# Gate products of a gated graph network: one Strassen–Winograd step in fp32, or three float32r products of split operands

## The chip, the cores and the metric

The kernel runs on one core of one Trainium2 chip. The metric is the device time of one execution in microseconds; the kernel before the change takes 2126.82 us, the median of 3 runs (2126.05 to 2127.76).

## What is computed

There are 128 graphs of 128 nodes with 256 features each. Two layers follow one another, both with a residual. Cut to what matters:

```
h = relu(layernorm(x))                          # first layer: gated graph network
A = (adj != 0)
for i in 0..2:                                  # three rounds
    aggr = A^T @ (h @ weight[i])
    gi = aggr @ w_ih.T + b_ih ; gh = h @ w_hh.T + b_hh      # 768 columns: r, z, n
    r = sigmoid(gi_r + gh_r) ; z = sigmoid(gi_z + gh_z)
    n = tanh(gi_n + r * gh_n)
    h = (1 - z) * n + z * h
x = x + h
h = relu(layernorm(x))                          # second layer: graph attention
Wh = h @ W.T
att = softmax over j of leaky_relu(Wh@a1 [i] + Wh@a2 [j]) where adj, else 0
out = x + att @ Wh
```

The "gate products" are gi and gh. The kernel multiplies `weight[i]` into `w_ih` once, at the start, so a round needs (A^T h) times a product matrix and h times `w_hh`.

## The kernel before, in words

Four graphs form a group (G = 4, T = 512 node columns), so there are 32 groups of three rounds, and a **step** is one round of one group. State is kept turned, as `hT`: 2 chunks of 128 features by 512 columns. The 96 steps are in an order written out at the end (`plan`, L1152), sorted by 3·group + STEP·round with STEP = 4, so that two to three steps of other groups lie between two rounds of one group. The last step of all is done in two halves of 256 columns.

What a step does on each engine:

- **gather** (`inputs`, L647, and `gathered`, L630): the state in rows, `h`, times the mask A gives `pa` in PSUM: 8 fp32 products of 128 columns; ScalarE copies `pa` to `aT` (L663).
- **moving sums** (`moving_sums`, L484): VectorE makes the four Winograd sums of `hT` and of `aT`, 8 operations of 128x256 (L493).
- **gate products** (`gru_step`, L710): the 256x256 products are cut in 2x2 blocks and done with 7 block products in place of 8 (`blocks`, L749, and `product`, L723). A step has two phases (reset gate with the hidden half of the new state; update gate with the given half). Each phase has 7 products of 3 matmuls, so a step issues 42 fp32 matmuls of 128x128 by 256 columns, all on L737. Between the products ScalarE copies PSUM banks (L757, L760, L770) and VectorE adds them (L763, L774).
- **gates**: tanh and scaling on ScalarE from PSUM (L795, L802, L830), additions on VectorE (L837, L682), tanh of the new state (L688), then the new state in three VectorE operations of 128x1024 (L694, L696, L698).
- **rows**: the next gather needs the state in rows. Where more than two steps lie between rounds, VectorE transposes 32x32 blocks and SyncE's queue moves them through DRAM (`to_rows_by_blocks`, L581, `by_way_of_dram`, L538); otherwise TensorE transposes (`rows`, L618, `to_rows`, L519).

After the third round the `epilogue` (L940) does the attention of that group: `pq` (L637) and `po` (L1124) on TensorE and the rest on the other engines. The `prologue` (L905) normalises a group's input.

The order of all instructions is set when the program is built. `Order` (L173) keeps a time for each engine; work that is not a gate product waits as tasks, each with an assumed length, and `fill`, `fixed` and `matmuls` place the tasks around the products. Once placed, each engine runs its instructions in that order and waits for what they need. SyncE issues every DMA (L60).

At the start the product matrices are computed (`given_weights`, L368) and their Winograd sums made (`stationary_sums`, L328).

Of the kernel before, what the change touches and what calls it, by code (L numbers as in the profile page):

```python
# [8 lines left out]
F32 = mybir.dt.float32  # L9
I32 = mybir.dt.int32  # L10
# [13 lines left out]
BIG = 1e30  # L24


@with_exitstack
def preln_gnn_kernel(
# [33 lines left out]
    XT, AT = 3, 2  # L62
    ROWS = 6
# [6 lines left out]
    def load_adjacency(g):  # L70
        at = io.tile([P, G, P], I32, tag="at", name=f"at_{g}", bufs=AT)
        dma(at, adj[g * G : (g + 1) * G].rearrange("b s t -> s b t"))
        return at
# [15 lines left out]
    def two_chunks(pool, tag, name, **bufs):  # L89
        return [borrowed(pool, [P, C, T], tag, f"{name}_{k}", 3 * D, **bufs) for k in range(C)]  # L90

    wih = two_chunks(work, "hs", "wih")
    whh = two_chunks(gate, "v", "whh")
# [7 lines left out]
    def load_weight(l, pool, shape, tag):  # L101
        w = borrowed(pool, shape, tag, f"wt_{l}", C * D)
        w = w.rearrange("p (c d) -> p c d", d=D)
        dma(w, weight_t[l].rearrange("(c p) d -> p c d", p=P))
        wt.append(w)


    load_weight(0, gate, [P, 2, H], "m")
    load_gates(wih, w_ih_t, slice(0, 1))
# [3 lines left out]
    xts, ats = {0: (xt_0, (4.8, 5.8))}, {}  # L113
    load_gates(wih, w_ih_t, slice(1, 3))
    ats[0] = load_adjacency(0), 8.6
    load_gates(whh, w_hh_t, slice(0, 1))
    load_gates(whh, w_hh_t, slice(2, 3))
    load_gates(whh, w_hh_t, slice(1, 2))
    load_weight(1, work, [P, G, P], "e")
    load_weight(2, work, [P, G, P], "e")  # L120
# [7 lines left out]
    gw = borrowed(work, [P, G, P], "prT", "gw", C * D).rearrange("p (c f) -> p c f", f=D)  # L128
# [3 lines left out]
    for g in range(2, XT):  # L132
        xts[g] = load_rows(g), 18.0 + 2.0 * g
# [6 lines left out]
    c1 = [ps_sum.tile([P, 2, H], F32, name=f"c1_{n}") for n in range(2)]  # L140
    c2 = ps_sum.tile([P, 2, H], F32, name="c2")
    u = ps_sum.tile([P, 2, H], F32, name="u")
    m7 = ps_sum.tile([P, 2, H], F32, name="m7")
    for bank in (*c1, c2):
        bank = bank.rearrange("p g t -> p (g t)")
        put(nc.tensor.matmul(bank, zero[:, 0:P], zero, start=True, stop=True))
# [24 lines left out]
    more = u, m7, c2, *c1  # L171

    class Order:  # L173
        def __init__(self):
            self.free = dict.fromkeys((PE, ACT, DVE, POOL, SP, "port"), 0.0)
            self.tasks = []

            self.rooms = {room: [0.0] * 2 for room in ("tq", "x1", "prT", "e", "hs")}
            self.rooms |= {"misc": [0.0] * 3, "h": [0.0] * ROWS}
            self.next, self.room_of = dict.fromkeys(self.rooms, 0), {}  # L180
# [37 lines left out]
        def open(self, room, name):  # L218
            self.room_of[name] = room, self.next[room]
            self.next[room] = (self.next[room] + 1) % len(self.rooms[room])  # L220
            if room == "misc" and self.room_of[name][1] > 2:

                return more[self.room_of[name][1] - 3].rearrange("p n t -> p (n t)")
            if room == "misc":
                return ps_misc.tile([P, T], F32, tag="misc", name=name)
            if room == "h":
                return work.tile([P, G, D], F32, tag="h", name=name, bufs=ROWS)
# [4 lines left out]
            return work.tile([P, C, T], F32, tag=room, name=name)  # L232
# [90 lines left out]
    S1, S2, S3, S4, N22, W11, W12 = range(7)  # L323

    def stationary_tile(name):
        return const.tile([P, 3, 7, P], F32, name=f"s_{name}")

    def stationary_sums(s, into, w, gates, ready):  # L328


        v = [wk.rearrange("p (g o m) -> p g o m", g=3, o=2) for wk in w]
        w11, w21 = v[0][:, gates, 0, :], v[0][:, gates, 1, :]
        w12, w22 = v[1][:, gates, 0, :], v[1][:, gates, 1, :]
        n = gates.stop - gates.start
        eng = nc.vector
        long, short = 0.05 + 0.15 * n, 0.05 + 0.12 * n

        def done(block, t):
            for gate_no in range(gates.start, gates.stop):
                into[gate_no, block] = t  # L340

        t = yield DVE2, long, ready
        put(eng.tensor_tensor(s[:, gates, S3, :], w11, w21, ALU.subtract))
        done(S3, t)
        t = yield ACT, 0.1 + 0.14 * n, ready
        put(nc.scalar.copy(s[:, gates, W11, :], w11))
        done(W11, t)
        t1 = yield DVE2, long, ready
        put(eng.tensor_tensor(s[:, gates, S1, :], w21, w22, ALU.add))
        done(S1, t1)  # L350
        t = yield ACT, 0.1 + 0.14 * n, ready
        put(nc.scalar.copy(s[:, gates, W12, :], w12))
        done(W12, t)
        t2 = yield DVE2, long, t1 - HOP
        put(eng.tensor_tensor(s[:, gates, S2, :], s[:, gates, S1, :], w11, ALU.subtract))
        done(S2, t2)
        t = yield DVE, short, ready
        put(eng.tensor_scalar(s[:, gates, N22, :], w22, -1.0, None, ALU.mult))
        done(N22, t)
        t = yield DVE2, long, t2 - HOP  # L360
        put(eng.tensor_tensor(s[:, gates, S4, :], w12, s[:, gates, S2, :], ALU.subtract))
        done(S4, t)

    def hidden_weights(gates):
        for g, ready in gates:
            yield from stationary_sums(s_hh[0], s_hh[1], whh, slice(g, g + 1), ready)

    def given_weights(l, wf, pieces):  # L368


        for gates, ready in pieces:
            n = gates.stop - gates.start
            cols = slice(gates.start * D, gates.stop * D)
            for c in range(C):
                t = yield PE, 0.86 * n, ready, "misc"
                pw = order.open("misc", f"pw_{l}_{c}_{gates.start}")
                for k in range(C):
                    put(nc.tensor.matmul(  # L378
                        pw[:, 0 : n * D], wt[l][:, k, c * P : (c + 1) * P], wih[k][:, cols],
                        start=(k == 0), stop=(k == C - 1),  # L380
                    ))
                t = yield (ACT, 0.07 + 0.28 * n, t) if c else (DVE, 0.08 + 0.3 * n, t)
                order.close(f"pw_{l}_{c}_{gates.start}", t)
                if isinstance(wf[0], tuple):
                    wf[:] = [
                        borrowed(pool, shape, tag, f"wf_{l}_{k}", 3 * D, bufs=bufs)
                        for k, (pool, shape, tag, bufs) in enumerate(wf)
                    ]
                copy = nc.scalar.copy if c else nc.vector.tensor_copy
                put(copy(wf[c][:, cols], pw[:, 0 : n * D]))  # L390
            yield from stationary_sums(s_f[l][0], s_f[l][1], wf, gates, t)
# [9 lines left out]
    def score_weights(ready):  # L401
# [15 lines left out]
        t = yield PE, 0.5, t, "misc"  # L417
        pr = order.open("misc", "pw_r")
# [42 lines left out]
    def norm_apply(src, graphs, rstd, nb, ready, name, kept, room="h"):  # L461

        for k in graphs:
            t = yield (ACT, 0.5, ready) if kept else (ACT, 0.5, ready, room)
            if not kept:
                h = order.open(room, f"h_{name}")
                if room == "tq":
                    h = h.rearrange("p c t -> p (c t)").rearrange("p (k d) -> p k d", d=D)
                kept.append(h)
# [6 lines left out]

    def columns_tile(tag, name):
        return work.tile(
            [P, C, T], F32, tag=tag, name=f"{tag}_{name}", bufs=7 if tag == "hT" else 2
        )  # L480

    T1, T2, T3, T4 = range(4)

    def moving_sums(X, into, ready, name, parts):  # L484


        t = work.tile([P, 4, H], F32, tag=f"t{name[0]}", name=f"t_{name}")
        sums = [t[:, i, :].rearrange("p (a w) -> p a w", a=parts) for i in range(4)]
        x = X.rearrange("p c (a n w) -> p c a n w", a=parts, n=2)
        x11, x21, x12, x22 = (x[:, c, :, n] for n in range(2) for c in range(2))  # L490
        for i, one, other in ((T3, x22, x12), (T1, x12, x11), (T2, x22, sums[T1]), (T4, sums[T2], x21)):
            into[i] = t, (yield DVE2, 0.34, ready)
            put(nc.vector.tensor_tensor(sums[i], one, other, ALU.subtract))  # L493

    def to_columns(h, ready, name):
# [11 lines left out]
        for c, pt in enumerate(banks):  # L507
            t = yield ACT, 0.57, ready
            order.close(f"pt_{name}_{c}", t)
            if hT is None:  # L510
                hT = columns_tile("hT", name)
# [46 lines left out]
    def to_columns_by_blocks(h, ready, name):  # L558
# [14 lines left out]
        def place():  # L573
            nonlocal hT
            hT = columns_tile("hT", name)
            return hT.rearrange("p c t -> p (c t)")

        t = yield from by_way_of_dram(tmp.rearrange("p q n a -> p (q n) a"), place, C * G, t, name)
        return hT, t

    def to_rows_by_blocks(hT, ready, name):  # L581

        tmp = None
        for c in range(C):
# [8 lines left out]
            ))  # L593
        h = None
# [23 lines left out]
    def rows(s, ready, name):  # L618
# [3 lines left out]
        for half, pt in enumerate(banks):  # L622
            t = yield (ACT, 0.57, ready) if half else (ACT, 0.57, ready, "h")
            order.close(f"pr_{name}_{2 * half}", t)
            if h is None:
                h = order.open("h", f"h_{name}")
# [20 lines left out]
    def inputs(s, ready):  # L647

        name = f"{s.g}_{s.l}"
        s.tH, s.tA = {}, {}  # L650
        parts = len(s.parts())
        s.hidden = order.add(0, moving_sums(s.hT, s.tH, ready, f"h_{name}", parts))
        if s.l and not s.by_blocks():
            s.h, s.h_ready = yield from rows(s, ready, name)
        banks, ready = yield from gathered(s.h, s.A, s.h_ready, f"pa_{name}")
        order.close(f"h_{name}" if s.l else f"h_a{s.g}", ready)
        aT = None
        for c, pa in enumerate(banks):
            t = yield ACT, 0.57, ready
# [630 lines left out]
```

## Time and profile before

| what | value |
|---|---|
| median of 3 runs | 2126.82 us (2126.05 to 2127.76) |
| the profiled execution's own span | 2124.5 us |
| TensorE busy, weight loads busy | 2116.6 us, 1886.8 us |
| VectorE busy, ScalarE busy | 1733.1 us, 1301.4 us |
| first gate product starts | 16.21 us |
| granted clock, mean | 1.000 |

"Busy" is the share of time in which at least one instruction of the engine was running, so the durations of instructions that overlap add up to more. One fp32 matmul stands as two records in this trace, each with its own weight load. A record's duration includes the time until its last column has passed, which overlaps the next record; what one costs in a stream is the distance between starts, called its pitch below.

### The profile page before, as it was taken

To read this page: it belongs to the slowest core of one execution; us is meant where nothing else is said; L and a number is where in the kernel's file an instruction comes from. 1 tells how busy PE (TensorE), PEld (TensorE's weight loads), DVE (VectorE), ACT (ScalarE), POOL (GpSimd) and SP (SyncE) were. 2 spreads that over 40 slices of the span, in tenths; PEclk is the share of its full clock that TensorE was granted. 3 is DMA by queue.
4 is the path that set the end of the run, shared out by engine and by line. 5 is a ranking of instruction groups with operands and counts; after the bars stand their busy time and mean duration, and the time that the engine had idled before them with its cause. 6 is when DMAs were issued, how large, how long until landed. Compare 5 with 4: busy or idle time off the path is not lost.

```text
span 2124.5 us, 32340 instructions
## 1 busy us (share of the span) xinstructions
PE 2116.6 (100%) x10865; PEld 1886.8 (89%) x10865; DVE 1733.1 (82%) x3771; ACT 1301.4 (61%) x2875; POOL 126.5 (6%) x200
## 2 busy tenths in 40 slices
PE   9999999999999999999999999999999999999999
PEld 7888888888888888888888888888888888888888
DVE  7778888888878888888888888888888888787777
ACT  5556666566656666666656666666666566665666
POOL 1000000000000000000000000000000000000000
PEclk9999999999999999999999999999999999999999
DMA  5334454554455444545344554445453544444311
GB/s 159 65 85 88 86 118 107 107 117 92 98 115 119 84 96 107 122 109 113 83 108 104 117 122 82 98 106 123 110 107 88 107 107 105 96 98 94 70 31 46
DMA packets 667975, 211.95 MB, mean 100 GB/s; under 512 B 578336, under 2 KB 644640, under 8 KB 667808
## 3 DMA queue, kind: packets, MB, share of 16 engines
q1 hardware_dynamic: 667808, 209.87, 44.3%
q8 instruction: 86, 1.41, 0.3%
q14 instruction: 81, 0.66, 0.1%
HBM read 121.91 MB, written 87.88 MB: 99 GB/s over the span
## 4 chain that ended last, share of the span: by engine, by line
PE 98%; DVE 1%; ACT 0%; DMA 0%; issue 0%; POOL 0%; SPq 0%; ACTq 0%; DVEq 0%
PE c L737 35%; PE u L737 35%; PE m L737 12%; PE pa L637 8%; PE po L1124 5%; PE pq L637 2%; PE pw L378 0%; DMA xt<-in_x 0%; PE c L1124 0%; PE u L1124 0%; ACT v L688 0%; PE c L637 0%; PE pr_o L527 0%; DVE st_a L440 0%; PE pr L527 0%; ACT e L1065 0%
## 5 line engine op out<-in xcount | busy, mean ns | idle before, releaser
L830 ACT ACTIVATE z<-c,brz 128x256 f32<-128x256 f32 (+1 forms) x388 | 186.2, 480 | 328.4 <-PE c L737 186.4
L737 PE MATMUL u<-t_h,s_hh 128*128 128x256 f32 (+1 forms) x1164 | 345.0, 378 | 0.9 <-DVE c L763 0.5
L737 PE MATMUL u<-t_a,s_f 128*128 128x256 f32 (+1 forms) x1164 | 312.3, 377 | 0.0
L737 PE MATMUL c<-aT,s_f 128*128 128x256 f32 (+1 forms) x1164 | 312.3, 377 | 0.0
L795 ACT ACTIVATE r<-c,brz 128x256 f32<-128x256 f32 (+1 forms) x388 | 175.3, 475 | 194.3 <-PE c L737 112.8
L763 DVE TENSOR_TENSOR c<-u,m 128x512 f32<-128x512 f32 (+1 forms) x194 | 134.6, 694 | 140.8 <-PE u L737 140.4
L737 PEld LDWEIGHTS u<-t_h,s_hh 128*128 128x128 f32 x1164 | 218.4, 190 | 31.3 <-ACT c L757 1.6
L737 PEld LDWEIGHTS c<-aT,s_f 128*128 128x128 f32 x1164 | 220.4, 190 | 28.9
L737 PEld LDWEIGHTS u<-t_a,s_f 128*128 128x128 f32 x1164 | 220.4, 190 | 29.0
L737 PE MATMUL c<-hT,s_hh 128*128 128x256 f32 (+1 forms) x780 | 229.8, 376 | 0.0
L837 DVE TENSOR_TENSOR v<-v,c 128x256 f32<-128x256 f32 (+1 forms) x388 | 153.6, 415 | 66.3 <-PE c L737 43.7
L770 ACT COPY c<-u 128x512 f32<-128x512 f32 (+1 forms) x194 | 109.7, 566 | 117.5 <-PE u L737 116.1
L760 ACT COPY m<-m 128x512 f32<-128x512 f32 (+1 forms) x194 | 112.7, 581 | 107.1 <-PE m L737 106.9
L802 ACT ACTIVATE v<-c,bhn 128x256 f32<-128x256 f32 (+1 forms) x388 | 173.0, 474 | 0.0
L737 PE MATMUL m<-t_h,s_hh 128*128 128x256 f32 (+1 forms) x582 | 172.3, 378 | 0.0
L737 PE MATMUL c<-t_h,s_hh 128*128 128x256 f32 (+1 forms) x582 | 172.1, 377 | 0.0
L737 PEld LDWEIGHTS c<-hT,s_hh 128*128 128x128 f32 x780 | 147.6, 190 | 19.2
L774 DVE TENSOR_TENSOR c<-u,m 128x512 f32<-128x512 f32 (+1 forms) x194 | 131.8, 679 | 37.9 <-ACT c L770 34.9
L737 PE MATMUL u<-aT,s_f 128*128 128x256 f32 (+1 forms) x582 | 156.2, 377 | 0.0
L737 PE MATMUL m<-t_a,s_f 128*128 128x256 f32 (+1 forms) x582 | 156.1, 377 | 0.0
L737 PE MATMUL c<-t_a,s_f 128*128 128x256 f32 (+1 forms) x582 | 156.1, 377 | 0.0
L757 ACT COPY c<-u 128x512 f32<-128x512 f32 (+1 forms) x194 | 109.8, 566 | 43.7 <-PE u L737 43.7
(164 smaller groups left out, 3928.4 us busy)
## 6 DMA issues: line engine op xcount, KB each, us to landing
z<-tq SPq DMA_DIRECT2D x248, 128.0 KB
h<-z SPq DMA_DIRECT2D x248, 128.0 KB
xt<-in_x SPq DMA_DIRECT2D x31, 512.0 KB
z_a<-tq_a SPq DMA_DIRECT2D x120, 128.0 KB
hT_a<-z_a SPq DMA_DIRECT2D x120, 128.0 KB
z_b<-tq_b SPq DMA_DIRECT2D x116, 128.0 KB
h_b<-z_b SPq DMA_DIRECT2D x116, 128.0 KB
x<-in_x SPq DMA_DIRECT2D x29, 512.0 KB
```

What stands on the lines that cost most here:

```text
L637: put(nc.tensor.matmul(pa[:, k * P : (k + 1) * P], h[:, k, c * P : (c + 1) * P], A[:, k, :], start=True, stop=True,))
L737: put(nc.tensor.matmul(to(q), S[0][:, gate_no, weight, :], moving, start=first and q == 0 and i == 0, stop=(i == len(ends) - 1), skip_grou ...
L757: put(nc.scalar.copy(c1[0][:, :, 0:W], u[:, :, 0:W]))
L760: put(nc.scalar.copy(m[:, :, 0:W], m7[:, :, 0:W]))
L763: put(nc.vector.tensor_tensor(c2[:, :, 0:W], u[:, :, 0:W], m[:, :, 0:W], ALU.add))
L770: put(nc.scalar.copy(c1[1][:, :, 0:W], u[:, :, 0:W]))
L774: put(nc.vector.tensor_tensor(c22[:, :, 0:W], u[:, :, 0:W], m[:, :, 0:W], ALU.add))
L795: put(nc.scalar.activation(r[:, o, cols], src, AF.Tanh, bias=brz[:, o : o + 1], scale=0.5))
L802: put(nc.scalar.activation(v[:, o, cols], src, AF.Identity, bias=bhn[:, o : o + 1], scale=0.5))
L830: put(nc.scalar.activation(z[:, o, cols], src, AF.Tanh, bias=brz[:, C + o : C + o + 1], scale=0.5))
L837: put(nc.vector.tensor_tensor(v[:, o, cols], v[:, o, cols], src, ALU.add))
L1124: put(nc.tensor.matmul(po[:, j, :], hs[:, c, k * P : (k + 1) * P], gwt[:, c, :], start=(c == 0), stop=(c == C - 1),))
```

## The change

The gate products are no longer done with the Winograd sums. Each operand is split in an upper part (rounded to float32r by scaling with 1 − 2⁻¹³ on the write), a rest, and a third plane ("apart") that combines both. For each of weights and states there are three planes, and a product is the sum of three float32r products: upper by upper, rest by rest and apart by apart, the first two summed in one PSUM bank, scaled by 1 + 2⁻¹² on the way to a second bank, where the third is added. The weights' planes are made once at the start, the states' planes in each step.

A step has eight blocks of 128 output features by 512 columns; four of them take both hidden and given operand. Each use of an operand is 3 planes by 2 chunks, so a step issues 72 float32r matmuls of 512 columns (L775 of the new kernel).

Around this: STEP goes from 4 to 2, the state in rows is always made by TensorE transposes (L499), at most 4 groups are open in place of 6, input rows are prefetched 2 deep in place of 3, the mask is made in the tile that the adjacency lands in, and tiles come from counted rooms. The third plane of a block is issued behind the first two planes of the next block (`order.behind`). Cut to its core:

```diff
-    XT, AT = 3, 2
-    ROWS = 6
+    XT, AT = 2, 2
+    COLUMNS, MASKS, PLANES = 4, 4, 10
+    ROWS = {"ha": 1, "hr": 1, "h": 2}
...
-    def stationary_sums(s, into, w, gates, ready):
+    def stationary_planes(s, into, k, src, gates, ready, bank=None, factor=1.0):
...
+        put(nc.scalar.activation(upper, src, AF.Copy, scale=BELOW * factor))
...
+        put(nc.vector.scalar_tensor_tensor(
+            apart, src, factor, upper.bitcast(F32), ALU.mult, ALU.subtract
+        ))
...
+        put(nc.vector.tensor_scalar(rest, apart.bitcast(F32), 1.0 / UNIT, None, ALU.mult))
...
+        put(nc.vector.scalar_tensor_tensor(
+            apart, upper.bitcast(F32), -UNIT, apart.bitcast(F32), ALU.mult, ALU.add
+        ))
...
-    def moving_sums(X, into, ready, name, parts):
...
+    def split_rest(into, name, upper, t, whole):
...
+        put(nc.vector.scalar_tensor_tensor(
+            apart, into[REST][0].bitcast(F32), -1.0 / UNIT, upper.bitcast(F32), ALU.mult, ALU.add
+        ))
...
+    def state_planes(s, into, name):
...
+            put(nc.scalar.activation(upper[:, c, :], hT[:, c, :], AF.Copy, scale=BELOW))
...
+            put(nc.vector.tensor_tensor(rest, hT, upper.bitcast(F32), ALU.subtract))
...
+    def sum_planes(s, into, name):
...
+        banks, ready = yield from gathered(s.h, s.A, s.h_ready, f"pa_{name[3:]}")
...
+            put(nc.scalar.activation(upper[:, c, :], pa, AF.Copy, scale=BELOW))
...
+                put(nc.vector.tensor_tensor(
+                    rest[:, c, :], pa, upper[:, c, :].bitcast(F32), ALU.subtract
+                ))
...
-                    put(nc.tensor.matmul(
-                        to(q), S[0][:, gate_no, weight, :], moving,
...
+                    passes += [(weight[:, k, i, out], tile_x[:, k, cols]) for k in range(C)]
+            for i, (weight, moving) in enumerate(passes):
+                put(nc.tensor.matmul(
+                    to, weight, moving,
+                    start=first and i == 0, stop=i == len(passes) - 1, skip_group_check=True,
+                ))
...
+        def finish_block(block, i, ready):
...
+            done = product(
+                gate_no, o, ends_of[ends], (APART,), bank, False, ready,
...
+                put(nc.vector.scalar_tensor_tensor(
+                    tile_["v"][:, o, cols], tile_["r"][:, o, cols], 1.0, gates_[i][:, 0:W], ALU.add, ALU.mult
+                ))
...
+        BLOCKS = (
+            (NEW, 0, "h"), (RESET, 0, "ha"), (NEW, 1, "h"), (RESET, 1, "ha"),
+            (UPDATE, 0, "ha"), (UPDATE, 1, "ha"), (NEW, 0, "a"), (NEW, 1, "a"),
+        )
...
+            done = product(
+                gate_no, o, ends_of[ends], (UPPER, REST), sums[b][:, 0:W], True, order.free_sum[b],
...
+            if by_dve:
+                t = order.fixed(DVE, add_t, max(ready, tile_["half", o]))
+                put(nc.vector.scalar_tensor_tensor(
+                    to, bank, 1.0 + UNIT, tile_["v"][:, o, cols], ALU.mult, ALU.add
+                ))
+            else:
+                t = order.take(ACT, copy_t, ready)
...
-    STEP = 4
+    STEP = 2
...
-    LIVE = 6
+    LIVE = 4
```

## The prediction

> **What bounds the kernel now.** I read the summary of the page first, then the chain of work that ended last, then single stretches.
>
> ```profile
> PE 2116.6 (100%) x10865; PEld 1886.8 (89%) x10865; DVE 1733.1 (82%) x3771; ACT 1301.4 (61%) x2875; POOL 126.5 (6%) x200
> ```
>
> TensorE is busy all the time. A busy matmul row alone doesn't prove a bound, since records overlap, so the chain must say it:
>
> ```profile
> PE 98%; DVE 1%; ACT 0%; DMA 0%; issue 0%; POOL 0%; SPq 0%; ACTq 0%; DVEq 0%
> PE c L737 35%; PE u L737 35%; PE m L737 12%; PE pa L637 8%; PE po L1124 5%; PE pq L637 2%; PE pw L378 0%; DMA xt<-in_x 0%; PE c L1124 0%; PE u L1124 0%; ACT v L688 0%; PE c L637 0%; PE pr_o L527 0%; DVE st_a L440 0%; PE pr L527 0%; ACT e L1065 0%
> ```
>
> 98% of the chain is TensorE, 82% the gate products of L737. The pitch comes from the chain over 899 to 960 us (start, length, what):
>
> ```profile
> 918.34 1.29 PE u L737 x6
> 919.64 1.78 PE pa L637 x16
> 921.42 1.30 PE m L737 x6
> 922.72 1.78 PE pq L637 x16
> ...
> 928.39 2.59 PE c L737 x12
> 930.98 1.73 PE po L1124 x8
> ```
>
> No gap between the pieces. Twelve records of L737 take 2.59 us: 215.8 ns each, 431.6 ns for one fp32 matmul of 256 columns (two records). A 128-column record costs 1.78 / 16 = 111 ns.
>
> **What is removed on TensorE.** 95 full steps x 42 matmuls x 2 records = 7980 records of 256 columns (the sum of the groups of that form), at 215.8 ns: 1722.1 us. The two half steps are 168 records of 128 columns at 111 ns: 18.7 us. Total 1740.8 us.
>
> **What is added.** 95 x 72 = 6840 float32r passes of 512 columns, and 144 of 256. The trace has no float32r. Its rows bound a pass from both sides:
>
> - Low end: an fp32 matmul costs 431.6 ns for 256 columns in two records. If an fp32 product is four part products (two parts of each operand), a product of operands that are already short needs a fourth: 512 columns in 215.8 ns.
> - High end: every record of 4-byte data here, the TensorE transposes too, takes as long per column as an fp32 record: eight transposes of 128 columns fill 2061.59 to 2062.47 us, 110 ns each. At that rate 512 columns cost 431.6 ns.
>
> I take 215.8 ns. The nearest row is the one record type with short operands, the three bf16 products of 512 columns at the very start (L146): 610 to 635 ns each, where fp32 records of 512 columns (L378) last up to 987 ns in the early part and 592 ns later. So one record can stream a column in fewer cycles than fp32 does, and the splitting in upper part and rest leaves each operand short. Then 6840 x 0.2158 = 1476.1 us, and the halves 144 x 0.111 = 16.0 us: 1492.1 us. The gates gain 1740.8 - 1492.1 = **248.7 us**. Less than a fourth of the fp32 cost I exclude: nothing is left to drop.
>
> The Trainium skill's page "FP8 and Floating Point Precision", section "TensorE Precision Notes", does say that true fp32 takes four passes through the array, one for each pairing of high and low parts; by it a single pass would come to the low end, and no run here shows a single pass of a 4-byte operand.
>
> Weight loads: each pass loads its own 128x128 weights. A load lasts 190 ns (median of L737) and is hidden now: one stands for each record, PEld is busy 89%, and the pitch stays 215.8 ns; with 128-column records the pitch is even 111 ns. So: nothing.
>
> A rule of the Trainium skill speaks against that. The page "TensorE: Matmul & The Clock Gate", section "The mechanism", says that a weight load overlaps a running matmul only where their row groups differ. All these use all rows, so by that rule, with the same page's 107 ns for 128 columns, 6840 loads would add about 730 us (an estimate), and the change would lose. The gapless rows above disagree with it, and I go by them.
>
> **The state in rows** now always comes from TensorE: 512 transposes in place of 16, 496 x 0.110 = 54.6 us added. What leaves is two VectorE block transposes (L590, 0.70 us each) and eight DMAs for 62 of 64 rows; these lay off the chain, so they give nothing.
>
> Everything else on TensorE (pa, pq, po, the weights) has the same count. Net on TensorE: -248.7 + 54.6 = **-194.1 us**.
>
> **VectorE.** Per step before: 8 x 0.42 (L493) + 4 x 0.69 (L763, L774) + 4 x 0.417 (L837) + 1.22 (L682) + 3.65 (the three 128x1024 state operations), 12.7 us. After: 6 operations of 128x512 with a PSUM source (0.69, as L763) + 3 plane operations of 128x1024 (1.22, as L682) + 3.65 = 11.5 us. With the L590 transposes gone, VectorE has about 2 us less per step of some 20 us: its share stays near 82%. **ScalarE** per step: before 6 copies x 0.57, 12 x 0.477, 2 x 0.716, 2 x 0.583 = 11.7 us; after 6 copies at 0.57 (low, a COPY) to 0.716 (high, an ACTIVATE of that size), 6 tanh at 0.716 or less, four plane writes at about 0.6 and the row copies: 11 to 12 us. Neither becomes the bound: each has less work than TensorE in every step.
>
> **Where waiting comes in.** Now TensorE idles only 1.05 us between 16.21 and 2098.10 us. The change has tighter couplings.
>
> - *First and last round.* STEP = 2 puts (group 0, round 1) directly behind (group 0, round 0), and (31, 2) directly behind (31, 1); with STEP = 4 another step lies between. With nothing between, TensorE waits for the whole tail of the step: drain 0.16 (a record lasts 0.38 us at a pitch of 0.216) + tanh 0.72 + state 3.65 + upper planes 2 x 0.6 + rest 1.22, 7 us; the reset gate then waits for transposes, copies, gather and planes, about 2 us of it uncovered. **9 us** at the start. At the end the rows are transposed first and the upper planes run beside them: 0.16 + 0.72 + 3.65 + about 2.5: **7 us**. Little else is ready there.
> - *Head.* VectorE makes three operations per weight piece: 12 pieces of 128x256 (0.42 + 0.29 + 0.42) and 6 of 128x512 (0.69 + 0.42 + 0.69), 24 us, against some 17 us for the Winograd sums and copies that the first rows list (0.2 to 0.69 us each). 0 to 7 us; I take **4**, since part falls beside ScalarE and products.
> - *Each step.* The last two blocks (new state, given half) go from the first bank to the second by VectorE (0.69 us) where the ScalarE copy was free. Behind the last of them TensorE has only one third plane (2 x 216 ns) and the first block of the next step (4 x 216 ns), 1.29 us in all; the addition needs 0.16 + 0.69 + some 0.1. If VectorE has a 1.22 us operation running (a plane or state operation stands directly ahead in half of the steps of the new program), the wait shows on TensorE, and everything in TensorE's queue behind it waits, too. Bounds: 0 (as now) and one whole operation, 1.22 us. I take 0.3 us for 93 steps: **28 us**, nearer to zero, since the present kernel waits nowhere with the same VectorE share.
>
> Sum: 2124.5 - 194.1 + 9 + 7 + 4 + 28 = 1978 us of span. The median of the runs shown is 2.3 us above that span, so **1981 us**, 6.9% faster.
>
> **Rivals.**
>
> 1. *Nothing waits in the steps* (0 for 28, and a head without the 4): 1978 - 32 + 2 = 1949 us. For it: 82% VectorE share now without a gap. Against: half as many steps between rounds, and a 1.29 us cover.
> 2. *VectorE's additions wait for one full operation each step*: 93 x 1.22 = 113 us in place of 28: 1981 + 85 = 2066 us. For it: VectorE runs strictly in order and the planes come in pieces of 1.22 us. Against: the order places them with the addition's time in view.
> 3. *Slower than before: a float32r pass streams at the rate of an fp32 record*, in L775. 431.6 in place of 215.8 ns: 6840 x 0.2158 = 1476 us more, waits vanish: about 3430 us. It decides from a pitch of 0.2158 + (2126.8 - 1981) / 6840 = 0.237 us upwards; that is also where the change would fail to do what it says. For it: no 4-byte record in this trace goes faster. Against: the bf16 records, and that four part products in fp32 fall to one.
>
> Waits alone would have to reach (2126.8 - 1981 + 28) / 93 = 1.87 us in every step to eat the gain, more than a whole VectorE operation.
>
> **How the numbers follow.** The forecast, 1960 to 2010 us: 0.55. Rival 1, 1935 to 1960: 0.14. Rival 2, 2010 to 2090: 0.19. Between 2090 and 2122 us: 0.03; within 0.2%, which is about what a measurement of this kernel can tell from no change: 0.01. Rival 3 (0.07) and a loss by waits (0.01): 0.08. So faster 0.91, same 0.01, slower 0.08. The range 1942 to 2072 us takes in rivals 1 and 2 with the bounds of the waits and leaves out rival 3, about 2 in 10.
>
> **What will show it.** In the profile after: the pitch of L775 passes (12 in 2.59 us if right; 5.2 us for rival 3); PE records of L775 6984 in number, one each; PE's share of the chain still above 90%; 512 transposes at L499 with 110 ns; idle time of TensorE before the third planes, released by VectorE's L869, near 28 us for the forecast and near 100 us for rival 2; two gaps of 7 to 9 us, one in the first 60 us and one some 40 us ahead of the end. The prediction is wrong if loads of weights show between passes, if a plane (L650, L669, L697) and not the addition releases TensorE, or if ScalarE's scaled copies take so long that the banks come late.

## The result and the profile after

The changed kernel takes 2185.51 us (median of 4 runs, 2184.07 to 2188.61), the kernel before 2126.64 us in the same session: a ratio of 1.0278 with a 95% interval of 1.0263 to 1.0293. It is **slower by 2.8%**; 1981 us was forecast, with a range of 1942 to 2072. The profiled execution has a span of 2183.6 us and a mean granted clock of 0.973, where before it was 1.000.

The summary of the page and its chain of work, where before TensorE had 100% and 98%:

```profile
PE 2076.8 (95%) x10197; PEld 1738.4 (80%) x10197; DVE 1585.9 (73%) x2877; ACT 1270.5 (58%) x2409; POOL 96.0 (4%) x200
PE 87%; DVE 5%; DMA 3%; ACT 2%; SPq 2%; issue 1%; ACTq 0%; DVEq 0%
PE sum L775 45%; PE gate L775 23%; PE pa L612 8%; PE po L1139 5%; PE pr L499 3%; PE pq L612 2%; SPq L63 2%; DMA hT_a<-z_a 2%; DVE xh L669 1%; ACT xh L663 1%; DVE xa L697 1%; PE pw L376 1%; ACT r L790 0%; DVE v L832 0%; ACT v L800 0%
```

TensorE has fewer instructions, but 13% of the chain is now elsewhere, and among the rest stands a transfer, `hT_a<-z_a`, that neither a term nor a rival had. Two readings say where the time went.

**The pitch.** Pieces of the chain between 900 and 960 us (start, length, what):

```profile
904.89 1.81 PE sum L775 x8
...
908.98 1.81 PE sum L775 x8
```

Eight passes in 1.81 us are 226 to 227 ns each, not 215.8. Longer stretches give 226.8 ns (the 62 passes from 899.90 to 913.97 us take 226.9 each); with that, 6840 passes cost 75.2 us more than forecast.

**The waits.** All waits of TensorE, by what ended them (us in total, times, the longest):

```profile
PE sum L775 <- ACT xh L663: 55.1, 15, 5.2
PE pw L376 <- DVE s_f L341: 9.6, 1, 9.6
PE sum L775 <- DVE xh L669: 8.6, 15, 0.8
PE pw L376 <- DMA wih<-in_w_ih_t: 5.9, 1, 5.9
PE sum L775 <- DVE xa L697: 5.7, 15, 0.4
```

Further down the same answer has the wait to which the prediction gave 28 us:

```profile
PE gate L775 <- DVE gate L869: 1.1, 3, 0.4
```

One of the 15 waits for L663 is the first round near 67 us, as forecast. The other 14 stand where the first step of a group begins, some 132 us apart, at every second group, and last 3.3 to 4.0 us each. One of them, in the chain:

```profile
913.05 0.92 PE gate L775 x4
914.00 0.70 ACT r L790
914.72 0.69 DVE v L832
915.41 0.35 DVE st_a L433
...
916.17 0.62 DVE prT L585
916.81 0.55 SPq L63
...
919.66 3.00 DMA hT_a<-z_a
...
922.76 1.16 ACT xh L663 x2
923.94 1.24 DVE xh L669
...
925.22 1.22 PE sum L775 x2
926.44 3.41 PE pa L612 x16
```

The group's first state comes back from DRAM turned (`hT_a<-z_a`) at 922.66 us, its upper planes are written behind it, and only then can TensorE go on. Two passes then take 1.22 us in place of 0.45, and 16 products of the gather 3.41 in place of 1.78. The windows say why (length; busy time of PE, PEld, DVE, ACT, POOL with counts; granted clock; DMA share; GB/s):

```profile
916.00:920.00 4.00, 3.85 (x18) 2.85 (x16) 3.06 (x6) 2.46 (x6) 1.45 (x3) 1.00 0.38 74
920.00:924.00 4.00, 0.53 (x2) 0.23 (x2) 2.70 (x6) 3.38 (x11) 0.00 (x0) 1.00 0.94 215
924.00:928.00 4.00, 3.52 (x12) 2.81 (x13) 2.64 (x4) 0.66 (x1) 0.00 (x0) 0.50 0.72 140
928.00:932.00 4.00, 3.79 (x16) 3.05 (x15) 0.53 (x1) 1.25 (x3) 0.00 (x0) 0.65 0.62 97
```

TensorE idles for 3.5 of 4 us, and then the granted clock is 0.50 for some 7 us: a wait is paid for again behind itself. Over the whole span, TensorE idles for 106.8 us (before: 7.9). The time lost to the clock while TensorE was running (1 minus the granted clock, times its busy time, summed over windows of 1 us) is 49.2 us (before: 0).

### The profile page after: what moved, and what is told of

The parts are those of the page before. It is cut to its first block, busy times and chain, and to the rows that moved or that the text cites. A ratio compares the mean times of both kernels' runs of the same rounds, so it can differ in the third digit from the quotient of the medians.

```text
span 2183.6 us, 28993 instructions
## 1 busy us (share of the span) xinstructions
PE 2076.8 (95%) x10197; PEld 1738.4 (80%) x10197; DVE 1585.9 (73%) x2877; ACT 1270.5 (58%) x2409; POOL 96.0 (4%) x200
## 4 chain that ended last, share of the span: by engine, by line
PE 87%; DVE 5%; DMA 3%; ACT 2%; SPq 2%; issue 1%; ACTq 0%; DVEq 0%
PE sum L775 45%; PE gate L775 23%; PE pa L612 8%; PE po L1139 5%; PE pr L499 3%; PE pq L612 2%; SPq L63 2%; DMA hT_a<-z_a 2%; DVE xh L669 1%; ACT xh L663 1%; DVE xa L697 1%; PE pw L376 1%; ACT r L790 0%; DVE v L832 0%; ACT v L800 0%
## 5 line engine op out<-in xcount | busy, mean ns | idle before, releaser
L775 PE MATMUL sum<-xh,s_hh 128*128 128x512 f32 (+1 forms) x2328 | 651.2, 400 | 63.9 <-ACT xh L663 55.1
L775 PE MATMUL sum<-xa,s_f 128*128 128x512 f32 (+1 forms) x2328 | 637.4, 393 | 10.8 <-DVE xa L697 5.7
L775 PEld LDWEIGHTS sum<-xh,s_hh 128*128 128x128 f32 x2328 | 437.1, 191 | 167.8 <-ACT xh L663 65.9
L775 PEld LDWEIGHTS sum<-xa,s_f 128*128 128x128 f32 x2328 | 431.1, 188 | 114.3 <-DVE xa L697 16.2
L879 ACT ACTIVATE gate<-sum 128x512 f32<-128x512 f32 (+1 forms) x388 | 224.1, 578 | 321.9 <-PE sum L775 303.9
L775 PE MATMUL gate<-xh,s_hh 128*128 128x512 f32 (+1 forms) x1164 | 369.7, 399 | 0.0
L775 PE MATMUL gate<-xa,s_f 128*128 128x512 f32 (+1 forms) x1164 | 364.7, 395 | 1.2 <-DVE gate L869 1.1
L869 DVE SCALAR_TENSOR_TENSOR gate<-sum,v 128x512 f32<-128x512 f32 (+1 forms) x194 | 134.4, 693 | 187.8 <-PE sum L775 174.6
L775 PEld LDWEIGHTS gate<-xa,s_f 128*128 128x128 f32 x1164 | 219.1, 191 | 47.1 <-DVE gate L869 2.9
L775 PEld LDWEIGHTS gate<-xh,s_hh 128*128 128x128 f32 x1164 | 212.9, 188 | 39.5 <-issue 1.0
L734 DVE TENSOR_TENSOR hT_a<-hT_a,v 128x1024 f32<-128x1024 f32 (+1 forms) x97 | 117.3, 1209 | 92.5 <-ACT v L800 92.5
L669 DVE TENSOR_TENSOR xh<-hT_a,xh 128x1024 fp32r<-128x1024 f32 x96 | 116.8, 1217 | 57.8 <-ACT xh L663 57.6
L663 ACT ACTIVATE xh<-hT_a 128x512 fp32r<-128x512 f32 x192 | 113.7, 625 | 52.8 <-DVE hT_a L738 46.1
L697 DVE TENSOR_TENSOR xa<-pa,xa 128x512 fp32r<-128x512 f32 x192 | 122.9, 681 | 4.7 <-ACT xa L687 4.7
```

The source lines that it names most:

```text
L663: put(nc.scalar.activation(upper[:, c, :], hT[:, c, :], AF.Copy, scale=BELOW))
L669: put(nc.vector.tensor_tensor(rest, hT, upper.bitcast(F32), ALU.subtract))
L697: put(nc.vector.tensor_tensor(rest[:, c, :], pa, upper[:, c, :].bitcast(F32), ALU.subtract))
L775: put(nc.tensor.matmul(to, weight, moving, start=first and i == 0, stop=i == len(passes) - 1, skip_group_check=True,))
L869: put(nc.vector.scalar_tensor_tensor(to, bank, 1.0 + UNIT, tile_["v"][:, o, cols], ALU.mult, ALU.add))
L879: put(nc.scalar.activation(to, bank, AF.Copy, scale=1.0 + UNIT))
```

## The experiments

What each kernel leaves out or changes stands in its expectation; the first is the only one that does not compute the whole.

**e1_pace: a pass by itself.** Only matmul series, 240 matmuls each with 128x128 weights: float32r with 512, 256, 128 and 384 columns, fp32 with 256, bf16 with 512.

> The kernel computes nothing of the reference: it issues runs of 240 matmuls, one shape and type after the other, with every other engine idle. Theory 'the pass itself': a float32r pass has a fixed extra of 13 ns over its columns, whatever runs beside it: 512 columns at a pitch of 227 ns, 384 at 173, 256 at 120, and with the same weights each time no change. Rival 'company': the 227 ns of the changed kernel come from the other engines' traffic, and alone a pass of 512 columns takes 216 ns as an fp32 record does. Rival 'the load': the extra is the float32r weight load not hidden behind a pass; then bf16 passes of 512 columns, with their shorter loads, stay at 216 ns, and 128 columns of float32r cost far more than 67 ns. fp32 of 256 columns should repeat 431.6 ns for its two records.

Windows inside the series of float32r with 512 columns, float32r with 256, fp32 with 256, bf16 with 512, and float32r with 512 and the same weights in every pass:

```profile
24.00:72.00 48.00, 48.00 (x214) 39.73 (x213) 0.00 (x0) 0.00 (x0) 0.00 (x0) 1.00 0.00 1
78.00:102.00 24.00, 24.00 (x202) 24.00 (x201) 0.00 (x0) 0.00 (x0) 0.00 (x0) 1.00 0.00 1
108.00:204.00 96.00, 96.00 (x447) 84.50 (x446) 0.00 (x0) 0.00 (x0) 0.00 (x0) 1.00 0.00 1
214.00:256.00 42.00, 41.79 (x193) 19.04 (x195) 0.00 (x0) 0.00 (x0) 0.00 (x0) 1.00 0.00 1
266.00:310.00 44.00, 44.00 (x196) 36.45 (x195) 0.00 (x0) 0.00 (x0) 0.00 (x0) 1.00 0.00 0
```

A window counts about two records more than fit, since those at its ends are cut. So a float32r pass of 512 columns takes 48 / 212 = 226.4 ns with all other engines idle; the chain, 231 records in 52.35 us, gives 226.6. An fp32 record takes 96 / 445 = 215.7 ns, as in the kernel before, and the bf16 series lasts 51.75 us for 240, 215.6 ns. The 11 ns belong to the float32r pass itself, not to the company of other engines. They are no rate per column either: 256 columns take 120 ns and 384 take about 173, so a pass of these widths is about 0.415 ns per column and some 13 ns on top.

Whether the weight load makes these 13 ns stays open. Against it speaks the fp32 series, which hides loads as long (84.50 / 446 = 189 ns) under records of 215.7 ns. But the series with the same weights still issues a load for every pass (195 loads), so it takes none away. And both signs that were named for the rival 'the load' came: bf16, with loads of about 98 ns (19.04 / 195), stays at 215.6 ns, and 128 columns of float32r take 111 ns, not 67. No run has a float32r pass without its load. What the sum needs, the price of a pass, is measured all the same.

**e2_turn_pe: the first state turned by TensorE.** It takes the DRAM round trip out of the prologue:

```diff
-        transposed = to_columns if g < 2 else to_columns_by_blocks
+        transposed = to_columns
```

> The first state of every group is turned by TensorE (8 transposes, 2 ScalarE copies), not by way of DRAM; the order is made anew. Theory 'late first state': the 15 waits of about 5 us for the first state's upper plane, and the half clock that follows each, vanish; 30 x 0.87 us of transposes are added: 2185 - 99 (steady idle and slow clock: 15 x (4.8 + 3.5) = 125 less 26) = about 2085 us, the clock back to 0.99 or more. Rival 'the order is too tight': the waits move to another operand, and the time stays above 2150 us.

2081.14 us, ratio 0.9783 (0.9767 to 0.9800). The waits are gone but for the one near 67 us:

```profile
PE sum L775 <- ACT xh L663: 5.2, 1, 5.2
```

The way over DRAM in the prologue of every second group is what TensorE waits for. But TensorE does 240 more transposes, and the edit makes the whole order anew, so it doesn't say *why* the prologue is late.

**e3_pool: another queue for the reads.** The turned first state is read back through GpSimd's queue:

```diff
-            dma(to_[q * 32 : (q + 1) * 32], rows_[q])
+            put((nc.gpsimd if name[0] == "a" else nc.sync).dma_start(to_[q * 32 : (q + 1) * 32], rows_[q]))
```

> Only the four DMAs that bring the turned first state back from DRAM are issued by GpSimd's queue in place of SyncE's; the order on TensorE, VectorE and ScalarE is that of the changed kernel. Theory 'queue': these reads are late because they stand in SyncE's queue behind writes of another group's attention that wait for VectorE (L585). Freed of that, they come up to 4 us earlier, most of the 15 waits go: 2080 to 2110 us. Rival 'late start': the write to DRAM itself starts too late, or the round trip is too long; then the waits stay and the time is 2160 to 2190 us, or longer, if GpSimd's queue is slower.

2199.57 us, ratio 1.0343 (1.0324 to 1.0362); the waits for L663 are 72.3 us, longer than with SyncE's queue. But the edit did not free the reads: in GpSimd's queue they stand behind operations on `norm_a` (L447 to L451) that themselves wait for VectorE. In the late groups they start 7.2 us behind the first write to DRAM, in the changed kernel 7.1. So this run leaves the theory untested. What the queue costs can be bounded with the next kernel: there the reads of most groups start 5.5 us behind the first write, so the queue could account for some 1.6 us (an estimate) of a wait of 3.3 to 4.0.

**e4_pass: the assumed duration of a pass.** The order of all instructions is made with an assumed 0.2165 us per pass; here it has the measured number. The kernel computes the same with the same instructions in another order:

```diff
-        copy_t, act_t, add_t, pass_t = (0.57, 0.72, 0.69, 0.2165) if part is None else (0.37, 0.48, 0.42, 0.12)
+        copy_t, act_t, add_t, pass_t = (0.57, 0.72, 0.69, 0.2268) if part is None else (0.37, 0.48, 0.42, 0.12)
```

> Only the assumed length of a pass in the order is changed, from 0.2165 to the measured 0.2268 us. Theory 'late first state by the queue': the order around the waits changes by chance, the mechanism stays; the time is within 30 us of 2185. Rival 'wrong assumption': the waits exist because the order reckons with passes 5% too fast; with the right length the waits shrink by half or more and the time falls below 2130 us.

2054.57 us, ratio 0.9663 (0.9649 to 0.9677): my theory of that moment fell. One number in the ordering, and the change is 3.4% *faster* than the kernel before. All 14 waits are gone; of the waits for L663 the one near 67 us is left:

```profile
PE sum L775 <- ACT xh L663: 5.2, 1, 5.2
```

What differs is when SyncE issues the load of an adjacency matrix. In the changed kernel, loads start at 813.18, 892.66, 920.12 and 1025.29 us: steps of 79.5, 27.5 and 105.2, two of them close together. In e4_pass they start at 830.21, 891.76, 953.25 and 1014.81, 61.5 us apart. VectorE's rows of the changed kernel show what each of them waits for:

```profile
891.94 0.69 DVE L1069 TENSOR_TENSOR e<-e,A 128x512 f32<-128x512 f32 x1
906.98 0.42 DVE L943 TENSOR_SCALAR A<-A 128x512 f32<-128x512 int32 x1
...
918.74 0.69 DVE L1069 TENSOR_TENSOR e<-e,A 128x512 f32<-128x512 f32 x1
```

and SyncE's:

```profile
892.66 0.38 SPq L63 DMA_DIRECT2D A<-in_adj  x1
...
911.07 2.98 SPq L63 DMA_DIRECT2D z_a<-tq_a  x4
...
918.21 1.88 SPq L63 DMA_DIRECT2D hT_a<-z_a  x4
920.12 0.42 SPq L63 DMA_DIRECT2D A<-in_adj  x1
```

L1069 adds an older group's mask to its attention scores and is the last use of that mask's tile. The next adjacency load follows within 0.1 us of its end at 892.63 (the one after 919.43 within 0.7 us, behind the reads in SyncE's queue), since the mask is made in the tile in which the adjacency lands and there are four. With that matrix a group is admitted (`admit`, at most four open); its mask is made at 906.98 (L943), its state written out at 911.07 and read back from 918.21 on. The theory from this, **late admission**: when attentions come in pairs, so do free tiles and admissions, and one group of each pair is late; and the late group makes the next attentions a pair again. Its rival: the wrong number itself makes the waits. The rows show the order of events, not how the lateness splits: from the load to the first write 18.4 us pass in the late groups, 17.0 in e4_pass. Five kernels test the theory.

**e5_admit: more room, the number left wrong.**

```diff
-    COLUMNS, MASKS, PLANES = 4, 4, 10
+    COLUMNS, MASKS, PLANES = 4, 5, 10
...
-            pending and not waiting and len(live) < LIVE
+            pending and not waiting and len(live) < (LIVE + 1 if pending[0] < 28 else LIVE)
```

> One mask tile more (5 instead of 4) and, up to group 27, one more open group (5 instead of 4); the assumed 0.2165 us of a pass is left as it is. Theory: the period-2 waits come from late admission: a group's prologue starts only when its adjacency matrix has a tile, and that tile is still held by the mask of an older group. Then the twelve waits before the first states of groups 4 to 26 go, each some 5 us idle and about 4 us of lowered clock behind it: 2185 - 12 x 8.5 = about 2083, within 2070 to 2105, and the waits of groups 28 and 30 stay. Rival: the assumed duration alone makes the waits, whatever room there is: the waits stay and the time is within 20 us of 2185.

2086.55 us, ratio 0.9809 (0.9792 to 0.9825), with 2083 expected. Waits for L663:

```profile
PE sum L775 <- ACT xh L663: 23.9, 3, 15.2
```

Twelve of the 14 are gone; the longest, 15.2 us at 1750 us, stands where the extra group is no longer allowed. From 376 to 1727 us the adjacency loads now come 60 to 62 us apart, as in e4_pass, though the number is the wrong one.

**e9_masks and e10_live: each half alone.**

> Only the fifth mask tile of e5_admit, still four open groups. Theory: the two limits bind at the same place, so that one alone frees nothing: within 20 us of 2185, with the fourteen waits left. Rival: the held tile is the whole cause: 2070 to 2110.

> Only the fifth open group of e5_admit (up to group 27), still four mask tiles. Theory: the adjacency matrix of the late group still has no tile, so the waits stay: within 20 us of 2185. Rival: the number of open groups is the whole cause: 2070 to 2110.

2184.08 us (1.0266, 1.0249 to 1.0283) and 2186.06 us (1.0278, 1.0263 to 1.0293); both keep all 15 waits (e9_masks first):

```profile
PE sum L775 <- ACT xh L663: 54.8, 15, 5.2
PE sum L775 <- ACT xh L663: 58.0, 15, 5.2
```

The two limits bind together: a tile without a place among the open groups is worth nothing, and the other way round. Whoever had tried only one would have dropped the right theory.

**e7_p2060 and e8_p2235: a worse and a better wrong number.** Only `pass_t` is changed, to 0.2060 and to 0.2235.

> Only the assumed duration of a pass, 0.2060 us instead of 0.2165: further from the measured 0.227 than the changed kernel's. Theory: what decides is not how true the number is but whether the greedy order, with its four masks and four open groups, falls into the pattern in which every second group is admitted late; with 0.2060 the order shows no such pattern, only a short gap at every group, which the longer real passes cover: 2050 to 2110. Rival: a wrong number costs by how wrong it is: over 2185.

> Only the assumed duration of a pass, 0.2235 us: nearer to the measured 0.227 than the changed kernel's 0.2165. Theory (the pattern of late admission decides): with 0.2235 the order still admits every second group late, from group 5 on: 2140 to 2200, with waits some 125 us apart. Rival (the error of the number decides): 70 per cent of the error is gone, so the time is within 40 us of the 2054.6 of the run with 0.2268.

With 0.2235, near the truth, the time is 2148.21 us (1.0102, 1.0087 to 1.0117), and waits stay at twelve places besides the one near 67 us:

```profile
PE sum L775 <- ACT xh L663: 35.7, 13, 5.5
```

Eight of the twelve are only 1.3 us long, the other four 4.6 to 5.5.

With 0.2060, the worst number of all, it is 2136.64 us (1.0048, 1.0033 to 1.0063). That is outside what either theory said. The waits at every second group are gone, as mine had it (waits for L663: 5.2 us, once), but another wait comes, 31 times, once in nearly every group:

```profile
PE pa L612 <- ACT h L602: 37.9, 31, 1.3
```

I had expected the longer real passes to cover it, and they don't: in the chain around 933 us the next passes stand behind the planes of `xa` (L697), and these behind three state operations on VectorE (L734, L736, L738). With the time that shows as busy it costs (2136.6 - 2054.6) / 31 = 2.6 us a group. So the time does not follow the error of the number (0.2060: 2136.6; 0.2165: 2185.5; 0.2235: 2148.2; 0.2268: 2054.6); each number tips the order into another pattern, and only the even one is good. Whether 0.2268 is good because it is true, or by luck, four values can't say.

**e6_head: the first round.** With 0.2268, and the second rounds of groups 0 and 1 later in the order:

```diff
-    plan = sorted(((g, l) for g in range(NG) for l in range(NL)), key=lambda n: NL * n[0] + STEP * n[1])
+    plan = sorted(((g, l) for g in range(NG) for l in range(NL)), key=lambda n: {(0, 1): 3.5, (1, 1): 3.7}.get(n, NL * n[0] + STEP * n[1]))
```

> The assumed pass at the measured 0.2268 us, and second rounds of groups 0 and 1 placed later in the hand-given order, so that round 1 of group 0 no longer stands directly behind its round 0. Theory: the gap near 62 us (some 6 us idle and the lowered clock behind it) goes from the run with 0.2268 alone: 2054.6 - 8 = about 2046, within 2041 to 2051. Rival: what is moved only shifts the gap to the next round that has no cover: 2052 to 2060.

2045.94 us, ratio 0.9621 (0.9606 to 0.9635), 8.6 us less than e4_pass. The window of the gap, first in the changed kernel:

```profile
58.00:74.00 16.00, 9.91 (x38) 7.38 (x37) 8.54 (x9) 5.57 (x10) 0.00 (x0) 0.68 0.00 1
```

and in e6_head:

```profile
58.00:74.00 16.00, 16.00 (x81) 13.47 (x80) 13.60 (x24) 9.80 (x17) 1.44 (x3) 1.00 0.45 99
```

This is the best version, 3.8% faster than the kernel before.

## Why the prediction was wrong

The difference of 205.6 us between the forecast span of 1978 and 2183.6 closes:

| term | us | from |
|---|---|---|
| pass 226.8 in place of 215.8 ns, x 6840 | +75.2 | chain (e1_pace, alone: 226.4 to 226.6) |
| late first states, 14 places | +129.9 | span of the changed kernel less that of e4_pass, 2053.7 |
| all other waits: 28 + 9 + 7 + 4 forecast | -6.8 | idle 36.6 and clock 12.5 in e4_pass, less 7.9 idle before, is 41.2 |
| not explained | +7.3 | 1.3 of it the half steps: 144 passes of 256 columns at 120 in place of 111 ns |

- **The price of a pass ("I take 215.8 ns")** was mis-sized by 5%. The low end came from the fp32 record, and the bf16 rows that should support it were 610 to 635 ns long in the slow early part and could not. The row for the high end did not show a rate either: e1_pace's float32r passes of 128 columns take 111 ns, as the fp32 transposes do, and those of 512 take 226.6. I took a bound as the value. Alone this would have left 1981 + 75 = 2056 us; e4_pass, which has no late groups, measures 2054.6.
- **The waits were sought in the wrong place ("Each step").** The additions at L869 cost 1.1 us, not 28; the prediction's own sign of being wrong, that planes and not the addition release TensorE, came (L663 55.1, L669 8.6, L697 5.7 us). What failed is a missing term: the front part of the document lists four open groups in place of six, input rows two deep in place of three, and the mask made in the landing tile, and the prediction priced none of it. e5_admit, e9_masks and e10_live show that the mask tiles and the open groups together hold the late groups back; the input rows were not tried. The prediction said that the block transposes and DMAs of the rows "lay off the chain, so they give nothing"; those of a group's first state remained, and moved onto it. The loss is 129.9 / 14 = 9.3 us a place: 5.0 idle (106.8 - 36.6), 2.6 clock (49.2 - 12.5), and the remaining 1.7 stands in the windows as busy: from 931.5 to 933.9 the chain is not on TensorE, though its windows show little idle time.
- **The clock had no term.** In the profile before it was 1.000 throughout, with 7.9 us of idle time in all, and the sum has no term for it. In the changed kernel it falls behind the waits; in e4_pass, where TensorE idles for only 0.8 us between 80 and 1954 us, it is 1.00 there as well. The Trainium skill's page "TensorE: Matmul & The Clock Gate", section "HAM oscillation — how this bites in real kernels", warns of this: idle gaps above about 3.4 us bring the clock to half. The site above agrees (3.59 us idle, then 0.50), and a wait of 3.05 us in e4_pass near 2000 us left the clock at 1.00. But in e8_p2235 waits of 1.30 and 0.76 us, near 450 us, were followed by a mean of 0.57 over 4 us. Of the eight waits of 1.3 us there, six were followed by a mean of 0.61 to 0.74 over 6 us and two by 1.00, so the length of the wait in the records alone doesn't decide it.
- **First and last round (9 and 7 us)** were right in place, and the first in size: 5.2 us of wait at 67 us and the clock behind it, in e4_pass 9.5 us in all from 56 to 80 us; e6_head takes 8.6 us away. At the end the waits are near in size, 4.6 us (2119 us) and 2.8 us (2149 us), but with the clock and the idle time of the last attention the last 100 us of e4_pass lose 14.3 us against the kernel before.
- **The head (4 us)** was too small: the first 56 us of e4_pass lose 17.0 us against the kernel before. TensorE waits 9.6 us for a weight plane of L341. The operations are as long as counted; what was missed is their order. VectorE's rows show that pieces of another weight and, for 4.7 us, the statistics of later groups stand ahead of that plane (no run moves them):

```profile
25.50 0.43 DVE L349 SCALAR_TENSOR_TENSOR s_hh<-s_hh 128x256 fp32r<-128x256 f32 x1
25.84 0.42 DVE L433 BATCH_NORM_STATS2 st_a<-xt 128x6 f32<-128x256 f32 x1
...
30.49 0.17 DVE L439 TENSOR_SCALAR norm_a<-mv_a 128x4 f32<-128x4 f32 x1
30.57 0.42 DVE L341 SCALAR_TENSOR_TENSOR s_f<-pw,s_f 128x256 fp32r<-128x256 f32 x1
```

  TensorE also waits 5.9 us for `wih` (before: 1.4), whose load SyncE now starts at 3.74 us, behind input rows, hidden weights and an adjacency matrix, and before at 1.22.
- **The sum of the four guesses.** That they add up nearly to what e4_pass shows, 48 against 41, is luck: "Each step" was 27 us too high, and the head (17.0 for 4) and the last round (14.3 for 7) made most of it good.
- **Removed work, transposes and loads** were right: 6984 passes at L775, 512 transposes at L499, a pitch far from a pass plus a whole load (226.8 ns, loads of 187 to 190), VectorE (73%) and ScalarE (58%) no bounds. VectorE's share "near 82%" was a slip: 2 us less in each of 96 steps is 1541 of 1978 us, 78%.
- **The rivals.** Rival 3 had the right side with the wrong mechanism: the pitch rose to 0.2268, not beyond its 0.237. The sentence that waits alone would need 1.87 us in *every* step was true and misled: two mechanisms that were each too small came together, 75 + 130 against a margin of 146, and the waits were few and long, not many and short.

## What to carry to other kernels

A change that buys space or order with fewer buffers can have a second price in the steps *between* pieces of work; look for the resource that the next piece needs before it may start (here a mask tile and a place among the open groups), and follow it through the profile. When an order is made from assumed durations, measure the new operation by itself first: one number of 0.2165 decided between 3% slower and 3% faster, and not in proportion to its error. If every wait of an engine falls on the same line at a fixed distance, suspect a count of buffers, and change the counts together before giving the theory up.

## What was unexpected of the hardware

- A float32r pass is slower than a bf16 one of the same 512 columns, 226.6 to 215.6 ns, and not by a rate: 120 ns for 256 columns, about 173 for 384. With 128 columns it is 111 ns.
- The granted clock stays at 0.50 for several us behind a wait; in the changed kernel this adds 49.2 us to 106.8 us of idle time. Waits of 1.25 us in e7_p2060 left it at 1.00; of those of 1.30 us in e8_p2235 most did not.
